# Four graph layers on one core: last rows as narrow products, a group's maxima in one reduction, exponentials one step earlier, the last output in quarters

## The chip, the core and the metric

The kernel runs on one core of a Trainium2 chip. The core has a matrix engine (PE, with a separate row PEld for the loading of its stationary operand), a vector engine (DVE), a scalar engine (ACT), GpSimd (POOL), and queues that issue DMAs, here mostly SyncE's (SP) and POOL's. Each engine works through its own list of instructions in order; semaphores hold an instruction back until what it reads is written and what it overwrites has been read. The metric is the device time in microseconds (us) of one execution, given as the median of several runs.

## The reference, cut to what matters

A graph of N = 2708 nodes with F = 512 features goes through four layers, each followed by `x = layernorm(x + layer(x))`. Layer 0 is a four-head attention with two dense blocks, and the change leaves it alone. The other three are:

```
# layer 1: mean over neighbours
A = (adj != 0);  deg = sum(A, axis=0)
y = A @ (x @ W + b) / deg[:, None]
# layer 2: masked softmax of x's own products
node_att = softmax(x @ node_w, axis=0)
h = x @ edge_w;  e = where(adj > 0, h @ h.T, -9e15)
y = adj * (node_att * softmax(e, axis=1)) @ (x @ weight) + bias
# layer 3: attention with a bias
a = (x@Wq+bq) @ (x@Wk+bk).T / sqrt(512) + adj + adj
y = softmax(a, axis=-1) @ (x @ Wv + bv)
```

All arrays are float32. 2708 is 21 blocks of 128 rows and one last block of 20, and this block of 20 is what several parts of the change are about.

## The kernel before

**Blocks and groups.** `BLOCKS` holds the 22 row blocks. Layer 1 works on four output blocks at a time (five groups of four, then one of blocks 20 and 21); layers 2 and 3 on `GROUPS` of three, seven of them, of which the last has four blocks (384 + 20 = 404 columns). A plain float32 product is two MATMUL instructions in the trace, one after the other; a product of `F32R` (layer 1's) is one.

**Layer 1** (L1013 to L1059). For every output group and every one of the 22 blocks jt of the sum, a strip of the transposed adjacency is loaded to `raw` (five buffers), turned to 0 and 1 in `at` (L1037, DVE), and used as the stationary operand of two products per output block (L1044), with `hid_hi` and `hid_lo`, the upper and lower part of the hidden rows. In the last group the strip is only 148 columns wide; the kernel zeroes `raw` first (L1033) and uses all 128 columns of the last block, of which 20 are real. When a group's sums are done, L1054 scales them and adds the old rows; the layer norms of these rows are put into the next group's loop, one every fourth jt. Those of the last group (blocks 20 and 21) come right after the loop (L1058).

**Between layers 1 and 2.** `quarters`, a small matrix that adds up four quarters of 32 partitions each, is made by 12 DVE additions (L1074 to L1083). Then layer 2's keys `hT` and values `sup` are projected group by group (L1430 to L1466), starting with transposes of the rows (L1095) that DVE copies out of PSUM (L1098).

**Layers 2 and 3** share `softmax_layer`. A step is one group and one block jt of keys. `one_score` loads the adjacency strip, makes the scores (L1203, 8 MATMULs; in layer 2, scores whose mirror image has been computed are transposed from a kept copy, L1195), masks or biases them on DVE into a tile `e` (L1497 or L1581) and takes the running maximum `mx` (L1251). For the block of 20 rows the four parts of the product go to four quarters of the array (L1227, `ps_parts`), are copied to SBUF (L1236) and added by a product with `quarters` (L1237). After a group's last score `spread_max` turns the maximum to one number per column: for each of the three or four blocks a transpose (L1263), a reduction (L1266) and a product with the identity (L1269), then a product with ones (L1274, `pb`) and a copy to `nmax` (L1287).

`one_sum` follows a score by `lag` = 25 steps: it adds `nmax` (L1294, DVE), takes the exponential (L1295, ACT), adds to the column sums `acc` (L1298 for the first block, a copy; L1305 for the others), in layer 2 multiplies by the adjacency, which is loaded again (L1500), and then gives `e` to PE for the output (L1310, in layer 2 six MATMULs; for the lonely last block L1339). After the last block `end` takes row sums of `acc` (L1360, `pr`), reciprocals (L1370) and, in layer 2, scales the result into the rows (L1505, L1506). `acc` has one buffer. Masks and adjacency strips share the five buffers of `a_cols`. The output sums take four PSUM banks in turn, three per group in layer 2.

In layer 3 `end` instead copies the sums out (L1356) and puts one `project` per output block into `later` (L1388, 8 MATMULs each), with `finish3` behind it: scale and add (L1587), layer norm (L102 to L112) and the store (L1592).

**Order.** A main loop (L1617 to L1634) calls, for each t, one score step, one sum step and one entry of `later`. Layer 3's scores start 12 steps after layer 2's have ended, so that for a while neither layer has a sum step. The instructions are not issued in this order alone: the framework plans ahead of time with estimated durations, gives every engine a fixed list, takes the earliest-written instruction that its plan holds to be ready, and adds the waits. Buffers with a tag are handed out in the order written, and a new use waits until the old one has been read.

Of the kernel before, what the change touches and what calls it, by code (L numbers as in the profile page):

```python
# [17 lines left out]
P = 128  # L18
# [11 lines left out]
def gnn_stack_kernel(  # L30
# [46 lines left out]
    rdeg = const.tile([P, NT], F32, name="rdeg")  # L77
    ones = const.tile([P, P], F32, name="ones")
    nc.vector.memset(ones, 1.0)

    def rows_tile(name):
        return big.tile([P, NT, F], F32, tag="rows", name=name)
# [863 lines left out]
    with (  # L946
# [66 lines left out]
        for g in range(0, NT, G):  # L1013
            group = range(g, min(g + G, NT))
            c0 = g * P
            w = min(N, c0 + G * P) - c0
            if g == G:
                ew_sb = load_weight(pw2, edge_w, "ew_sb")
                w2_sb = load_weight(pw2, w2, "w2_sb")
                nw_sb = load_row(pw2, node_w, "nw_sb")  # L1020
                b2_sb = load_row(pw2, b2, "b2_sb")
            pos = {
                it: psum.tile([P, F], F32, tag=f"po{it - g}", name="ps_nb", bufs=1 + (it - g < 2))
                for it in group
            }
            for jt, (j0, m) in enumerate(BLOCKS):
                if later and jt % 4 == 3:
                    y, n = later.pop(0)
                    layer_norm(y, y, n)
                raw = work.tile([P, G * P], F32, tag="raw", name="raw", bufs=5)  # L1030
                a = work.tile([P, G * P], F32R, tag="at", name="at", bufs=3)
                if m < P or w < len(group) * P:
                    nc.vector.memset(raw[:, : len(group) * P], 0.0)  # L1033
                for r in range(0, P if m == P else 2 * Q, P if m == P else Q):
                    nc.sync.dma_start(raw[r : r + m, :w], adjT[j0 : j0 + m, c0 : c0 + w])
                with tc.issue_after(ready[0].ins) if g == 0 and jt < 5 else nullcontext():
                    nc.vector.tensor_scalar(  # L1037
                        a[:, : len(group) * P], raw[:, : len(group) * P], 0.0, None, ALU.not_equal
                    )
                halves = (hid_hi, hid_lo) if m == P else (hid_hi,)  # L1040
                for it in group:
                    at = a[:, (it - g) * P : (it - g + 1) * P]
                    for k, half in enumerate(halves):
                        nc.tensor.matmul(  # L1044
                            pos[it],
                            at,
                            half[:, jt, :],
                            start=(jt == 0 and k == 0),
                            stop=(jt == NT - 1),
                        )  # L1050
            for it in group:
                n = BLOCKS[it][1]
                y = xs[:n, it, :]
                nc.vector.scalar_tensor_tensor(  # L1054
                    y, pos[it][:n], rdeg[:n, it : it + 1], y, ALU.mult, ALU.add
                )
                later.append((y, n))
        for y, n in later:  # L1058
            layer_norm(y, y, n)  # L1059

# [7 lines left out]
    GSPAN = [(g[0] * P, sum(BLOCKS[it][1] for it in g)) for g in GROUPS]  # L1070
    GW = max(w for _, w in GSPAN)
    GB = max(len(g) for g in GROUPS)

    quarters = featp.tile([P, C, Q], F32, name="quarters")  # L1074
    for c in range(C):
        nc.vector.tensor_tensor(
            quarters[:, c, :], ident[:, :Q], ident[:, Q : 2 * Q], ALU.add
        )
        for k in range(2, C):
            nc.vector.tensor_tensor(  # L1080
                quarters[:, c, :], quarters[:, c, :], ident[:, k * Q : (k + 1) * Q], ALU.add
            )
    quarters = quarters.rearrange("p c q -> p (c q)")  # L1083

    def key_tile(name):
        t = featp.tile([P, C, NFULL * P + Q], F32, tag="keys", name=name)
# [29 lines left out]
    def softmax_layer(  # L1116
# [12 lines left out]
        def key_order(gi):  # L1129

            late = list(range(NFULL // 2)) + [NT - 1] + list(range(NFULL // 2, NFULL))
            if not mirror:

                return late if gi else list(range(NT))
            early = [jt for jt in late if HOME[jt] < gi]
            late = [jt for jt in late if HOME[jt] >= gi]
            place = {jt: (k + 0.5) / len(early) for k, jt in enumerate(early)}
            place |= {jt: (k + 0.5) / len(late) for k, jt in enumerate(late)}
            return sorted(place, key=place.get)
# [113 lines left out]
        def spread_max(st):  # L1253

            gi = st["gi"]
            c0, w = GSPAN[gi]
            k = len(GROUPS[gi])
            tp = psum.tile([P, C, P], F32, tag="tp", name="tp_mx")
            nm = small.tile([P, GB], F32, tag="nm", name="nm")
            dg = att.tile([P, GB, P], F32, tag="dg", name="dg", bufs=1)  # L1260
            for b, it in enumerate(GROUPS[gi]):
                n = BLOCKS[it][1]
                nc.tensor.transpose(  # L1263
                    tp[:n, b, :], st["mx"][:, b * P : b * P + n], ident
                )
                nc.vector.tensor_reduce(  # L1266
                    nm[:n, b : b + 1], tp[:n, b, :], AX.X, ALU.max, negate=True
                )
                nc.vector.tensor_scalar(  # L1269
                    dg[:n, b, :n], ident[:n, :n], nm[:n, b : b + 1], None, ALU.mult  # L1270
                )
            pb = psum.tile([P, BANK], F32, tag="tp", name="pb")
            full = sum(BLOCKS[it][1] == P for it in GROUPS[gi])
            nc.tensor.matmul(  # L1274
                pb[:, : full * P],
                ones,
# [9 lines left out]
            st["nmax"] = att.tile([P, GW], F32, tag="nmax", name="nmax", bufs=2)  # L1286
            nc.scalar.copy(st["nmax"][:, :w], pb[:, :w])  # L1287

        def one_sum(st, k):
            gi, jt = st["gi"], st["order"][k]  # L1290
            c0, w = GSPAN[gi]
            j0, m = BLOCKS[jt]
# [1 line left out]
            nc.vector.tensor_tensor(e, e, st["nmax"][:, :w], ALU.add)  # L1294
            nc.scalar.activation(e, e, AF.Exp)  # L1295
            if k == 0:
                st["acc"] = att.tile([P, GW], F32, tag="acc", name="acc", bufs=1)
                nc.vector.tensor_copy(st["acc"][:, :w], e)  # L1298
                st["po"] = [
                    psum.tile([P, F], F32, tag=f"po{(GROUP * gi + b) % C}", name="po", bufs=1)  # L1300
                    for b in range(C if after is not None else len(GROUPS[gi]))
                ]
            else:
                acc = st["acc"][:m, :w]
                nc.vector.tensor_tensor(acc, acc, e[:m], ALU.add)  # L1305
            if weigh:
                weigh(e, load_a(gi, jt)[:, :w])

            def product(out, lhsT, rhs):
                nc.tensor.matmul(out, lhsT, rhs, start=(k == 0), stop=(k == NT - 1))  # L1310
# [37 lines left out]
        def end(st):  # L1348
# [19 lines left out]
            for b, it in enumerate(GROUPS[gi]):  # L1368
# [13 lines left out]
                if after is None:  # L1382
                    continue

                def project(b=b, it=it, n=n):
                    ps = psum.tile([P, F], F32, tag="tp", name="ps_o")
                    for c in range(C):
# [10 lines left out]

        states = {}

        def score_step(t):
            gi, k = divmod(t, NT)
            if k == 0:
                states[gi] = {"gi": gi, "e": [], "q": query(gi), "order": key_order(gi)}
            one_score(states[gi], k)
            if k == NT - 1:
                spread_max(states[gi])

        def sum_step(t):
            gi, k = divmod(t, NT)  # L1410
            if t == 0:
                last_values()
            one_sum(states[gi], k)
            if k == NT - 1:
                end(states.pop(gi))
# [10 lines left out]
    with (  # L1426
        tc.tile_pool(name="l2w", bufs=2) as work,
        tc.tile_pool(name="l2ps", bufs=4, space=PSUM) as psum,
    ):
        for gi, group in enumerate(GROUPS):  # L1430
            c0, w = GSPAN[gi]
            xt = work.tile([P, C, GW], F32, tag="xt", name="xt_g")
            for b, it in enumerate(group):
# [271 lines left out]
```

## Time and profile before

| what | value |
|---|---|
| median of 3 runs | 3321.99 us (3317.25 to 3322.62) |
| the profiled execution's own time | 3319.34 us |
| its span in the profile | 3317.5 us |
| PE busy | 3232.7 us (97%) |
| DVE busy | 1971.7 us (59%) |
| ACT busy | 1319.5 us (40%) |
| POOL busy | 130.1 us (4%) |

In the trace layer 1's sums run from 1293 to 1510 us of the span, the projections for layer 2 from 1511 to 1674, layer 2's steps from there to about 2398, and layer 3's from about 2310 to the end. The last MATMUL starts at 3311.4 us. A busy share is of the whole span; a MATMUL's duration includes its passage through the array, while the next one has already begun, so the distance between two starts tells more of PE than the duration. "Idle before" is the time the engine stood still before an instruction, and the arrow names the instruction that released it.

### The profile page before, as it was taken

The page shows a single profiled execution, that of the slowest core. Times are in us where ns is not written, and L with a number is a line of the kernel's source. Part 1 is how long each engine was busy: PE and PEld are TensorE (multiplying, and loading weights), DVE is VectorE, ACT ScalarE, POOL GpSimd, SP SyncE. Part 2 cuts the span into 40 slices and gives each one's busy share as a digit, 9 for nine tenths or more (in the row PEclk, how much of TensorE's full clock was granted, in tenths as well). Part 3 has the DMA queues.
Part 4 walks back from the last instruction along what each step waited for, and adds up shares of the span by engine and source line. Part 5 has one row for each costly group of instructions (what it writes and reads, how often), then busy time and mean ns, then how long its engine had stood idle before and what let it go on. Part 6 is the DMA issues. An engine that isn't in the chain of part 4 may idle for free.

```text
span 3317.5 us, 30401 instructions
## 1 busy us (share of the span) xinstructions
PE 3232.7 (97%) x10920; PEld 1725.2 (52%) x10920; DVE 1971.7 (59%) x3221; ACT 1319.5 (40%) x1497; POOL 130.1 (4%) x211
## 2 busy tenths in 40 slices
PE   8998999999999999999999999999999999999999
PEld 5443444454444446885554555444455555555554
DVE  7877977767687685445135667776353443543533
ACT  6887887457868652001133333332021010110111
POOL 1100100000000000000010000000000000000000
PEclk9999999999999999999999999999999999999999
DMA  8855863335555412540044444553211111111100
GB/s 289 299 189 169 310 214 123 105 108 199 177 176 175 161 40 84 144 123 15 1 127 128 119 124 134 148 148 108 69 46 34 42 34 42 40 32 45 36 24 20
DMA packets 172550, 381.45 MB, mean 115 GB/s; under 512 B 20938, under 2 KB 115094, under 8 KB 167982
## 3 DMA queue, kind: packets, MB, share of 16 engines
q1 hardware_dynamic: 156926, 308.16, 30.7%
q0 software_dynamic: 15472, 71.33, 5.8%
q8 instruction: 86, 1.41, 0.2%
q14 instruction: 66, 0.54, 0.1%
HBM read 307.22 MB, written 71.67 MB: 114 GB/s over the span
## 4 chain that ended last, share of the span: by engine, by line
PE 76%; DVE 9%; issue 8%; DMA 4%; ACT 3%; POOL 0%; SPq 0%; DVEq 0%; POOLq 0%; ACTq 0%
PE po L1310 22%; PE ps_s L1203 17%; PE po L460 11%; PE ps_nb L1044 6%; PE ps_wide L1105 4%; DVE t L393 3%; PE ps_hid L117 2%; PE ps_sup L1447 2%; PE ps_o L1388 2%; PE ps_mlp L713 2%; PE ps_dec L848 2%; DMA a<-adj_d 1%; ACT t L394 1%; DMA a_cols<-in_adjT_dram 1%; PE psm L483 1%
## 5 line engine op out<-in xcount | busy, mean ns | idle before, releaser
L393 DVE SCALAR_TENSOR_TENSOR t<-t,a 128x2708 f32<-128x2708 f32 (+1 forms) x156 | 462.1, 2974 | 125.0 <-ACT t L385 121.1
L385 ACT ACTIVATE t<-f1b,f2h 128x1354 f32<-128x1354 f32 (+1 forms) x312 | 428.1, 1413 | 61.7 <-PE po L460 28.0
L460 PE MATMUL po<-t,xw 128*128 128x452 f32 (+3 forms) x1056 | 415.1, 557 | 15.7 <-ACT t L394 15.7
L394 ACT ACTIVATE t<-t 128x2708 f32<-128x2708 f32 (+1 forms) x156 | 382.5, 2454 | 110.5 <-DVE t L393 110.3
L1310 PE MATMUL po<-sup,e 128*128 128x512 f32 x882 | 412.4, 602 | 6.2 <-DVE e L1500 5.9
L460 PE MATMUL po<-t,emb 128*128 128x452 f32 (+3 forms) x1056 | 400.3, 547 | 12.4 <-ACT t L394 9.1
L1310 PE MATMUL po<-e,xs 128*128 128x384 f32 (+1 forms) x1176 | 407.5, 489 | 0.0
L1203 PE MATMUL ps_s<-sup,hT 128*128 128x384 f32 (+1 forms) x1176 | 406.9, 490 | 0.0
L1581 DVE SCALAR_TENSOR_TENSOR e<-a_cols,ps_s 128x384 f32<-128x384 f32 (+1 forms) x154 | 85.6, 556 | 428.9 <-PE ps_s L1203 405.9
L460 PEld LDWEIGHTS po<-t,xw 128*128 128x128 f32 (+1 forms) x1056 | 191.2, 192 | 228.4 <-issue 201.7
L1203 PEld LDWEIGHTS ps_s<-sup,hT 128*128 128x128 f32 x1176 | 221.9, 190 | 164.2 <-issue 14.1
L460 PEld LDWEIGHTS po<-t,emb 128*128 128x128 f32 (+1 forms) x1056 | 193.5, 190 | 212.1 <-issue 187.3
L1310 PEld LDWEIGHTS po<-e,xs 128*128 128x128 f32 x1176 | 221.6, 190 | 157.2 <-issue 6.0
L1310 PEld LDWEIGHTS po<-sup,e 128*128 128x128 f32 x882 | 162.1, 192 | 173.9 <-issue 142.8
L1203 PE MATMUL ps_s<-hT 128*128 128x384 f32 (+5 forms) x672 | 212.3, 461 | 2.4 <-DVE e L1497 1.7
L97 ACT ACTIVATE ln_rstd<-ln_rstd 128x1 f32<-128x1 f32 x88 | 17.2, 201 | 495.0 <-DVE ln_rstd L96 494.7
L1496 ACT ACTIVATE a_cols<-a_cols,neg_big 128x384 f32<-128x384 f32 (+1 forms) x154 | 94.7, 616 | 239.0 <-DMA a_cols<-in_adjT_dram 190.7
L1044 PE MATMUL ps_nb<-hid_hi,at 128*128 128x512 f32 x484 | 185.6, 390 | 1.1 <-DVE at L1037 1.1
L1044 PE MATMUL ps_nb<-hid_lo,at 128*128 128x512 f32 x462 | 179.9, 389 | 0.0
L1305 DVE TENSOR_TENSOR acc<-acc,e 128x384 f32<-128x384 f32 (+2 forms) x294 | 162.4, 552 | 11.7 <-ACT e L1295 2.0
L1203 PEld LDWEIGHTS ps_s<-hT 128*128 128x128 f32 x672 | 122.4, 190 | 88.3 <-issue 17.3
L1294 DVE TENSOR_TENSOR e<-e,nmax 128x384 f32<-128x384 f32 (+1 forms) x308 | 154.5, 551 | 21.8 <-ACT nmax L1287 21.8
(247 smaller groups left out, 3316.8 us busy)
## 6 DMA issues: line engine op xcount, KB each, us to landing
a<-adj_d SPq DMA_DIRECT2D x110, 677.0 KB
a_cols<-in_adjT_dram SPq DMA_DIRECT2D x378, 192.0 KB
a<-in_adjT_dram SPq DMA_DIRECT2D x42, 677.0 KB
adj_d<-a POOLq DMA_DIRECT2D x42, 677.0 KB, 6.0
raw<-in_adjT_dram SPq DMA_DIRECT2D x105, 256.0 KB
kept<-t POOLq DMA_DIRECT2D x16, 1354.0 KB, 6.9
t<-kept SPq DMA_DIRECT2D x16, 1354.0 KB
a_cols<-in_adjT_dram SPq DMA_DIRECT2D x63, 202.0 KB
```

The costliest lines, as they stand in the source:

```text
L385: nc.scalar.activation(tv[:, k, :], f1b[:n, k, :w], AF.Tanh, bias=f2h[:n, jt, h : h + 1], scale=0.5,)
L393: step = nc.vector.scalar_tensor_tensor(tv, tv, GUARD, ab, ALU.add, ALU.mult)
L394: nc.scalar.activation(tv, tv, AF.Exp, scale=0.5)
L460: nc.tensor.matmul(po[HB * k + q][:, :qw], values[r : r + n, jt, h * P : (h + 1) * P], t[r : r + n, k, q0 : q0 + qw], start=(place == 0), ...
L1044: nc.tensor.matmul(pos[it], at, half[:, jt, :], start=(jt == 0 and k == 0), stop=(jt == NT - 1),)
L1105: nc.tensor.matmul(ps[:, :width], w(c, o), xt(c), start=(c == 0), stop=(c == C - 1),)
L1203: nc.tensor.matmul(ps[:, b * P : w], keys[:, c, j0 : j0 + P], st["q"][:, c, b * P :], start=(c == 0), stop=(c == C - 1),)
L1294: nc.vector.tensor_tensor(e, e, st["nmax"][:, :w], ALU.add)
L1305: nc.vector.tensor_tensor(acc, acc, e[:m], ALU.add)
L1310: nc.tensor.matmul(out, lhsT, rhs, start=(k == 0), stop=(k == NT - 1))
L1496: nc.scalar.activation(a, a, AF.Identity, bias=neg_big[: a.shape[0]], scale=1.0e30)
L1581: nc.vector.scalar_tensor_tensor(e, a, 2.0, ps, ALU.mult, ALU.add)
```

## The change

- **`quarters`** is made at the kernel's beginning, in the pool of constants, and no longer between layers 1 and 2.
- **Layer 1, last group.** `raw` is zeroed only for the last jt, `at` is made only as wide as the strip (148 columns), and block 21's products use its 20 columns as the stationary operand (128 rows by 20 columns) in place of 128.
- **Layer norms of blocks 20 and 21** after layer 1 are handed on as `last_rows` and issued before layer 2's second group of projections.
- **Key order of layer 3's first group:** the block of 20 comes last but one, not last.
- **`spread_max`:** all transposes first, then one reduction and one product with the identity for the full blocks together (and one of each for the block of 20). It is called after the first score of the next group; only the last group's comes straight after its last score.
- **`one_exp`** is split from `one_sum`: adding `nmax`, exponential, `acc` and the multiplication by the adjacency are issued for step t + 1 ahead of the products of step t, for the first step of a layer both. `acc` has two buffers.
- **Last output of layer 3:** block 21's projection is done in four quarters of the array (`project_parts`), copied by ACT and added by a product with `quarters` (`project_sum`); the order at the end becomes 18, parts of 21, 19, sum of 21, 20.

```diff
@@ constants @@
+    quarters = const.tile([P, C, Q], F32, name="quarters")
+    for c in range(C):
+        nc.vector.tensor_tensor(
+            quarters[:, c, :], ident[:, :Q], ident[:, Q : 2 * Q], ALU.add
+        )
...
@@ layer 1 @@
-                if m < P or w < len(group) * P:
-                    nc.vector.memset(raw[:, : len(group) * P], 0.0)
+                if m < P:
+                    nc.vector.memset(raw[:, :w], 0.0)
...
-                        a[:, : len(group) * P], raw[:, : len(group) * P], 0.0, None, ALU.not_equal
+                        a[:, :w], raw[:, :w], 0.0, None, ALU.not_equal
...
-                    at = a[:, (it - g) * P : (it - g + 1) * P]
+                    n = BLOCKS[it][1]
+                    at = a[:, (it - g) * P : (it - g) * P + n]
...
-                            pos[it],
+                            pos[it][:n],
...
-        for y, n in later:
-            layer_norm(y, y, n)
+        last_rows = later
@@ key_order @@
-                return late if gi else list(range(NT))
+                return late if gi else list(range(NFULL - 1)) + [NT - 1, NFULL - 1]
@@ spread_max @@
+            for b, count, n in [(0, full, P)] + [
+                (b, 1, BLOCKS[GROUPS[gi][b]][1]) for b in range(full, k)
+            ]:
+                some = slice(b, b + count)
                 nc.vector.tensor_reduce(
-                    nm[:n, b : b + 1], tp[:n, b, :], AX.X, ALU.max, negate=True
-                )
-                nc.vector.tensor_scalar(
-                    dg[:n, b, :n], ident[:n, :n], nm[:n, b : b + 1], None, ALU.mult
-                )
+                    nm[:n, some], tp[:n, some, :], AX.X, ALU.max, negate=True
+                )
+                nc.vector.tensor_tensor(
+                    dg[:n, some, :n],
+                    ident[:n, :n].unsqueeze(1).to_broadcast([n, count, n]),
+                    nm[:n, some].unsqueeze(2).to_broadcast([n, count, n]),
+                    ALU.mult,
+                )
@@ one_sum becomes one_exp and one_sum @@
-        def one_sum(st, k):
+        def one_exp(st, k):
...
-                st["acc"] = att.tile([P, GW], F32, tag="acc", name="acc", bufs=1)
+                st["acc"] = att.tile([P, GW], F32, tag="acc", name="acc", bufs=2)
                 nc.vector.tensor_copy(st["acc"][:, :w], e)
...
             if weigh:
                 weigh(e, load_a(gi, jt)[:, :w])
+
+        def one_sum(st, k):
...
@@ end, layer 3 @@
+                if it == NT - 1:
...
+                    def project_parts(b=b):
+                        ps = psum.tile([P, F], F32, tag="tp", name="ps_o4")
+                        for c in range(C):
+                            nc.tensor.matmul(
+                                ps[c * Q : (c + 1) * Q],
+                                oT[:, c, w - Q : w],
+                                after()[:, c, :],
+                                start=True,
+                                stop=True,
+                            )
+                        po = att.tile([P, F], F32, tag="values4", name="po4", bufs=1)
+                        nc.scalar.copy(po, ps)
+                        held.append(po)
+
+                    def project_sum(b=b, it=it, n=n):
+                        ps = psum.tile([P, F], F32, tag="tp", name="ps_o")
+                        nc.tensor.matmul(
+                            ps[:n], quarters[:, Q - REST : Q], held[0], start=True, stop=True
+                        )
+                        finish(it, ps[:n], rs[:n, b : b + 1])()
...
+                    before, last = later[-2:]
+                    later[-2:] = [project_parts, before, project_sum, last]
@@ score_step, sum_step @@
             one_score(states[gi], k)
-            if k == NT - 1:
+            if k == 0 and gi > 0:
+                spread_max(states[gi - 1])
+            if t == total - 1:
                 spread_max(states[gi])
...
             if t == 0:
                 last_values()
+                one_exp(states[0], 0)
+            if t + 1 < total:
+                one_exp(states[(t + 1) // NT], (t + 1) % NT)
             one_sum(states[gi], k)
@@ projections for layer 2 @@
         for gi, group in enumerate(GROUPS):
+            for y, n in last_rows if gi == 1 else ():
+                layer_norm(y, y, n)
```

## The prediction

> **What bounds the kernel now.** I read the page first.
>
> ```profile
> span 3317.5 us, 30401 instructions
> ...
> PE 3232.7 (97%) x10920; PEld 1725.2 (52%) x10920; DVE 1971.7 (59%) x3221; ACT 1319.5 (40%) x1497; POOL 130.1 (4%) x211
> ```
>
> PE is the bound and other engines count only where they make it wait, so an edit can earn in two ways: fewer or closer MATMULs, or a shorter PE wait. The chain of waits gives the steady distances: 8 MATMULs of 512 columns (L1388) in 3.43 us, 0.429 each; 32 of 384 (L1105) in 10.32, 0.322 each; 856 of layer 1's (L1044) in 194.59, 0.227 each. The width of the stationary operand is not in these numbers. Next, PE's own waits in 1670 to 2440 us (total, times, longest):
>
> ```profile
> PE po L1310 <- DVE e L1500: 5.9, 4, 3.9
> PE ps_s L1195 <- DVE e L1497: 2.3, 2, 1.9
> PE tp_mx L1263 <- DVE mx L1251: 1.7, 2, 1.3
> PE ps_s L1203 <- DVE e L1497: 1.7, 3, 0.9
> ```
>
> Few and small: what can be won is some 20 to 30 us of 3317. The timelines of PE and DVE show the longest one:
>
> ```profile
> 2282.13 0.72 PE L1360 MATMUL pr<-ones,acc 128*128 128x1 f32 x6
> 2286.78 3.78 PE L1310 MATMUL po<-sup,e 128*128 128x512 f32 x4 [3.93 <-DVE e L1500]
> ```
>
> ```profile
> 2283.32 2.06 DVE L1506 SCALAR_TENSOR_TENSOR xs<-po,rs,xs 128x512 f32<-128x512 f32 x3
> 2285.29 0.36 DVE L1298 COPY acc<-e 128x404 f32<-128x404 f32 x1
> ...
> 2286.17 0.56 DVE L1500 TENSOR_TENSOR e<-e,a_cols 128x404 f32<-128x404 f32 x1
> ```
>
> The next group's exponentials were long done, but `acc` has one buffer: its first copy must follow the old group's row sums (`pr`), DVE has put it behind L1506, and L1500 overwrites what the copy reads. PE then ran its next four MATMULs in 3.78 us, twice 0.429 apart: the wait also cost clock. The same view where layer 3's first maxima are taken:
>
> ```profile
> 2423.74 0.85 PE L1227 MATMUL ps_parts<-sup,hT 128*32 128x384 f32 x8
> 2425.19 0.91 PE L1237 MATMUL ps_s<-e,quarters 128*128 128x384 f32 x2 [0.60 <-ACT e L1236]
> 2427.42 0.30 PE L1263 MATMUL tp_mx<-ident,mx 128*128 128x128 f32 x1 [1.32 <-DVE mx L1251]
> ...
> 2430.09 1.62 PE L1274 MATMUL pb<-dg,ones 128*128 128x384 f32 x2 [0.80 <-DVE dg L1269]
> 2431.51 4.74 PE L1105 MATMUL ps_wide<-hT,mqk 128*128 128x384 f32 x8
> ```
>
> No sum steps exist here to fill PE, so each link of ACT, DVE and PE shows; again half clock follows. The step from layer 1 to 2:
>
> ```profile
> 1511.21 1.53 PE L1095 MATMUL tp<-ident,xs 128*128 128x128 f32 x12 [1.26 <-DVE xs L1054]
> 1515.32 1.98 PE L1447 MATMUL ps_sup<-w_sb,xt_g 128*128 128x512 f32 x4 [2.58 <-DVE xt_g L1098]
> ```
>
> Last, a place where a product with 20 columns stands between wide ones:
>
> ```profile
> 2399.88 0.91 PE L1203 MATMUL ps_s<-sup,hT 128*128 128x384 f32 x2
> 2400.72 1.03 PE L1376 MATMUL ps_po<-po,quarters 128*20 128x512 f32 x2
> 2401.68 8.01 PE L1203 MATMUL ps_s<-sup,hT 128*128 128x384 f32 x24
> ```
>
> The two L1203 lie between narrow products on both sides; they take 0.84 (2400.72 - 2399.88) in place of 2 x 0.322 = 0.64, and the narrow pair 0.96 in place of 0.86. Together 0.30 is lost for going narrow and back.
>
> **What the Trainium skill says.** "TensorEngine Tiling (Array Packing)", Key Properties: changing the tiling mode, not just the tile, drains the matrix engine. The trace agrees: start distances around L1376 and L1447's last block show +0.094 before a switch. "TensorE: Matmul & The Clock Gate", LDWEIGHTS: a load takes the operand's columns divided by 1.2, in ns, which would be 107 for 128 columns and 17 for 20 (estimates from that page); the trace has +0.105 on the first wide product after a narrow one and +0.014 on the first narrow one, so after a switch the load is not hidden. The same page, Part 1: an idle window halves PE's clock, and some 3.4 us of work restore it. After 2204 and 2286 the trace has doubled distances for 2.3 and 2.7 us in excess.
>
> **The change part by part.** Excess is the distance between two PE starts beyond the steady one.
>
> *Layer 1's narrow products.* The order per jt is wide, wide, narrow, narrow. 22 entries x (0.094 + 0.014) = 2.4; 21 returns x (0.093 + 0.105) = 4.2; together +6.5. No narrow F32R product is in the trace. Its distance could be a little below 0.227 (nothing is loaded for 108 columns; 43 x 0.01 = -0.4), and a switch might be hidden by F32R's single MATMUL, though L117, narrow, to L1044, wide, at 1292.99 shows the first F32R at 0.337 against 0.231 for those after it: +0.106. I take 0 for the first and the full switch. Bounds: -0.5 and +8. The 21 memsets that go (0.27 each, DVE) and narrower L1037 only help DVE; PE's two waits on it here (excess 0.69 at 1490.89, 0.76 at 1495.40) go, as a jt now lasts 1.2 us and not 0.9: -1.4. Sum **+5.1**.
>
> *Layer 1 to 2.* Between L1054's end (1511.2) and the first L1098 copy (1514.59) DVE does two layer norms and ten of the twelve small additions. Gone, the copy waits only for its four transposes (about 1511.8). PE needs its 12 transposes anyway (1.3 us); its 2.74 of excess shrink to near nothing. **-2.7** (bounds -1.5, -2.8). The wait for L1054 stays. The layer norms' new place is beside 19 us of PE work per group; uncovered they'd cost the same 2.7 again. The 12 additions at the start lie before 4.97 us, when PE's first product waits for a DMA, and the identity is there at 1.5: 0.
>
> *Group changes in layer 2.* Excess around the six changes: 0.3, 1.4, 1.3, 2.0, 6.2 (2204 to 2214, with half clock), 6.8 (2286 to 2292, likewise): 18.0. With two `acc` buffers and `one_exp` ahead, L1298 and L1500 of the new group stand before L1370, L1505 and L1506 on DVE; behind them wait only the scores' L1497 and PE's banks. What is late next: the new group's second product needs a bank that L1506's first (0.74, after 0.5 of small ones) frees, while PE has a score (0.33 to 2.6) and one product (0.86): about 0.5 per change, 3.0; and L1497, behind three L1506, still delays a score where scores are mere transposes, in three changes by about 1: 3.0. So -18.0 + 6.0 = **-12** (bounds -4, -17).
>
> *Maxima one score later.* Six small DVE operations of 0.29 become two, of which no row shows the shape; 384 elements are 0.55 in L1251, so 1.1 in place of 1.7. From transposes to L1500: transposes 0.5, reduce and product 1.1, `pb` 0.85, copy 0.48, L1294 0.55, L1295 0.52, L1298 0.35, L1500 0.55: 4.9, with queueing some 7. PE has three steps until it needs it (in the late groups 0.33 of L1195 and 2.57 of L1310 each, 8.7): hidden. At layer 2's first sums (1745, where L1500 was late by 1.27 already) scores alone cover it, and I charge **+1.5** (0 to +4).
>
> *Layer 3's first maxima.* Excess: 1.08 (L1237), 1.48, 0.58, 0.60, 1.17, then half clock 2.7: 7.6. Block 20's scores (2.6 us) now cover the ACT copy, L1105 and group 1's first score (12.9 us) the maximum. **-7.0** (bounds -4, -7.6). Layer 3's later groups have next to no excess: 0.
>
> *End.* 8 narrow MATMULs (3.43) become 8 in quarters, which in L1339 take 0.96, and 2 of the sum (0.86), plus a second switch 0.3: -1.2 on PE. But the last store has 128 rows: its packets end 1.66 us after issue, those of 20 rows 1.17: +0.5; and DVE has two blocks' chains (2.5 busy each) in the 4.6 us before the last one: +0.4. **-0.3** (-1.5, +1).
>
> Sum: 5.1 - 2.7 - 12 + 1.5 - 7.0 - 0.3 = -15.4. The execution profiled took 3319.34 (span 3317.5 and 1.8 around it): 3303.9. The median lies 2.65 above it: **3306.6**.
>
> **Rivals.** *The group changes keep their waits* (17 in 100): DVE's work there is nearly as much as before, and stalls at 1944, 2036 and 2123 name L1497, not L1500. Then layer 2 gives -2 and the sum is about -5: 3317. Against it: at 2286 no score is left, only L1500 holds PE. *The maxima come too late* (10 in 100, the slower side): slack falls from four steps to two before L1294. If the 7 us become 10 in late groups, and each of the six changes waits 3.5 and loses clock for 2.7 as at 2286, that is 37 in place of 18: +19, with the rest (-5) **3336**. It decides from about 3.8 us per change. For it: at 2272 to 2278 the way from first transpose to L1294 took 5.6. Against: a third of this was PE working on products between the single transposes, which the batch does away with. *More goes* (5 in 100): narrow switches hidden and all of layer 2's excess won, -26: 3296.
>
> **Numbers.** The likeliest case (68 in 100) has 3297 to 3315 by its bounds taken together. A measurement here tells about 0.2%, 6.6 us, from nothing: 3315.3 and 3328.6. Faster: 68 + 5 + a fifth of 17 = 0.76; same: the rest of 17, 0.14; slower 0.10. The range 3294 to 3321 leaves out the slow case and edges.
>
> **What will show it.** Layer 1's last group lasts 6 us longer, with first wide distances of 0.33; L1447 starts 1.3 us after L1095; no L1310 with idle over 1 us on L1500, no half clock after 2200; L1263 of layer 3's group 0 after L1105, without idle. Wrong if PE waits on `nmax`'s chain (L1294), if new rows of L1497 waits exceed 6 us, or if layer 1's last group keeps its 21 us.

## The result, and the profile after

| | before | after |
|---|---|---|
| median of 4 runs | 3321.31 us (3317.25 to 3322.62) | 3288.85 us (3285.64 to 3291.33) |
| the profiled execution's own time | 3319.34 us | 3290.97 us |
| its span | 3317.5 us | 3289.2 us |

The ratio is 0.9901, with an interval of 0.9888 to 0.9915: faster by 1%, some 32.5 us. The prediction had the direction, but 14.7 us of gain; the result lies below its range (3294). Nearest was the rival of 5 in 100, "more goes", with 3296.

The page of the kernel after has nearly the same PE work (11 us less busy time, two MATMULs more) in a span that is 28.3 us shorter (its last line here gives the share of each engine in the chain of work that ended last):

```profile
span 3289.2 us, 30359 instructions
...
PE 3221.7 (98%) x10922; PEld 1722.4 (52%) x10922; DVE 1944.6 (59%) x3144; ACT 1348.5 (41%) x1512; POOL 129.7 (4%) x211
...
PE 88%; DVE 5%; ACT 2%; DMA 2%; issue 1%; SPq 0%; DVEq 0%; ACTq 0%
```

Stages are compared by distances between two PE starts in the two traces. Layer 0 is the same work in both and scatters: 1204.8 us before, 1209.1 after, and from 1203.1 to 1209.1 over all kernels that are run below. So the comparison starts behind it, and from there on the two executions differ by 32.6 us, as the medians do.

| stage (from start to start of PE) | before | after | difference | predicted |
|---|---|---|---|---|
| layer 1, first five groups | 195.39 | 195.32 | -0.1 | 0 |
| layer 1, last group | 21.17 | 20.22 | -0.95 | +5.1 |
| layer 1's last product to layer 2's first score | 164.40 | 161.73 | -2.67 | -2.7 |
| from there to layer 2's first row sums | 167.84 | 166.40 | -1.44 | +1.5 |
| the six group changes of layer 2, row sums to row sums | 557.17 | 538.49 | -18.68 | -12 |
| layer 2's last row sums to layer 3's first sum | 55.16 | 47.93 | -7.23 | -7.0 |
| layer 3's sums | 842.59 | 841.44 | -1.15 | 0 |
| last sum to the end | 20.81 | 20.15 | -0.66 | -0.3 |

The six group changes, each with the sums of the group that follows, gave 0.19, 2.04, 2.46, 1.83, 6.16 and 6.00. PE's own waits in the stretch that answers to 1670 to 2440 of before (1670 to 2420 now; total, times, longest) name neither L1554 (the multiplication, L1500 before) nor L1264 (the transposes of the maxima, L1263 before):

```profile
PE ps_s L1237 <- ACT e L1236: 1.0, 1, 1.0
PE tp L1095 <- DVE ln_rstd L109: 0.7, 1, 0.7
...
PE ps_s L1203 <- DVE e L1551: 0.3, 1, 0.3
```

PE's timeline (start, busy time, instruction, output and operands, tiles, count) where layer 2's last group change was:

```profile
2268.79 0.72 PE L1374 MATMUL pr<-ones,acc 128*128 128x1 f32 x6
2269.38 5.40 PE L1324 MATMUL po<-sup,e 128*128 128x512 f32 x12
```

and DVE's there:

```profile
2267.64 0.56 DVE L1554 TENSOR_TENSOR e<-e,a_cols 128x404 f32<-128x404 f32 x1
...
2269.98 2.06 DVE L1560 SCALAR_TENSOR_TENSOR xs<-po,rs,xs 128x512 f32<-128x512 f32 x3
```

The next group's multiplications stand ahead of the old group's row sums. PE goes from `pr` straight into the next products, with twelve in 5.40 us; before it stood still for 3.93 and then ran four in 3.78. The bank that L1560 has yet to free costs at most 0.2 here: from the first of the twelve to the next product, at 2274.71, are 5.33 us, and 12 x 0.429 are 5.15. At the change before this one PE covers even that with the next score's transposes, which it puts between the group's first product and its second:

```profile
2193.33 0.72 PE L1374 MATMUL pr<-ones,acc 128*128 128x1 f32 x6
2193.92 0.69 PE L1195 MATMUL ps_s<-ident,s_kept 128*128 128x128 f32 x4
2194.53 1.13 PE L1324 MATMUL po<-sup,e 128*128 128x512 f32 x2
2195.50 0.49 PE L1195 MATMUL ps_s<-ident,s_kept 128*128 128x128 f32 x3
2195.82 1.88 PE L1324 MATMUL po<-sup,e 128*128 128x512 f32 x4
```

Where layer 3's first maxima are taken, the same view has three transposes between scores, all without idle time:

```profile
2402.61 0.91 PE L1105 MATMUL ps_wide<-hT,mqk 128*128 128x384 f32 x2
2403.36 0.83 PE L1237 MATMUL ps_s<-e,quarters 128*128 128x384 f32 x2
2404.03 2.74 PE L1203 MATMUL ps_s<-sup,hT 128*128 128x384 f32 x8
2406.61 9.84 PE L1105 MATMUL ps_wide<-hT,mqk 128*128 128x384 f32 x30
2416.28 2.74 PE L1203 MATMUL ps_s<-sup,hT 128*128 128x384 f32 x8
2418.86 0.49 PE L1264 MATMUL tp_mx<-ident,mx 128*128 128x128 f32 x3
```

From layer 1 to 2 only the wait for the last rows is left (the trace names a small memset of `hT` that DVE does as L1066, the scaling of these rows, ends). L1501 (L1447 before) starts 1.44 us after L1095, where it took 4.11:

```profile
1514.66 1.53 PE L1095 MATMUL tp<-ident,xs 128*128 128x128 f32 x12 [1.25 <-DVE hT L1087]
1516.10 1.98 PE L1501 MATMUL ps_sup<-w_sb,xt_g 128*128 128x512 f32 x4
```

And layer 1's narrow products, which the prediction charged for a switch of the array's mode at every change of width:

```profile
1495.80 0.39 PE L1056 MATMUL ps_nb<-hid_hi,at 128*20 128x512 f32 x1
1496.02 0.39 PE L1056 MATMUL ps_nb<-hid_lo,at 128*20 128x512 f32 x1
1496.25 0.39 PE L1056 MATMUL ps_nb<-hid_hi,at 128*128 128x512 f32 x1
1496.48 0.40 PE L1056 MATMUL ps_nb<-hid_lo,at 128*128 128x512 f32 x1
1496.72 0.39 PE L1056 MATMUL ps_nb<-hid_hi,at 128*20 128x512 f32 x1
```

Every distance shown is 0.22 to 0.24, whichever width comes next; the distance of 0.33 that was to follow each return isn't there. Over the whole group the only longer ones are the two at its single wait for DVE, at 1494.39 and 1495.23.

### The profile page after: what moved, and what is told of

Same layout as the page of the kernel before. It is cut to its first block, busy times and chain, and to the rows that moved or that the text cites. A ratio compares the mean times of both kernels' runs of the same rounds, so it can differ in the third digit from the quotient of the medians.

```text
span 3289.2 us, 30359 instructions
## 1 busy us (share of the span) xinstructions
PE 3221.7 (98%) x10922; PEld 1722.4 (52%) x10922; DVE 1944.6 (59%) x3144; ACT 1348.5 (41%) x1512; POOL 129.7 (4%) x211
## 4 chain that ended last, share of the span: by engine, by line
PE 88%; DVE 5%; ACT 2%; DMA 2%; issue 1%; SPq 0%; DVEq 0%; ACTq 0%
PE po L1324 23%; PE po L471 19%; PE ps_s L1203 18%; PE ps_nb L1056 6%; PE ps_wide L1105 4%; PE psm L494 3%; DVE t L404 2%; PE ps_hid L128 2%; PE ps_sup L1501 2%; PE ps_o L1432 2%; PE ps_mlp L724 2%; PE ps_dec L859 2%; DMA a<-adj_d 1%; ACT t L405 1%; ACT t L396 1%
## 5 line engine op out<-in xcount | busy, mean ns | idle before, releaser
L1302 ACT ACTIVATE e<-e 128x384 f32<-128x384 f32 (+1 forms) x308 | 151.7, 522 | 116.0 <-DVE e L1301 113.3
L1056 PE MATMUL ps_nb<-hid_hi,at 128*128 128x512 f32 x484 | 185.4, 390 | 0.4 <-DVE at L1048 0.4
L1056 PE MATMUL ps_nb<-hid_lo,at 128*128 128x512 f32 x462 | 179.9, 389 | 0.0
L108 ACT ACTIVATE ln_rstd<-ln_rstd 128x1 f32<-128x1 f32 (+1 forms) x88 | 17.2, 201 | 391.7 <-DVE ln_rstd L107 391.2
L1301 DVE TENSOR_TENSOR e<-e,nmax 128x384 f32<-128x384 f32 (+1 forms) x308 | 163.1, 552 | 23.3 <-ACT nmax L1294 23.3
```

Of the source, the lines that this page charges most:

```text
L1056: nc.tensor.matmul(pos[it][:n], at, half[:, jt, :], start=(jt == 0 and k == 0), stop=(jt == NT - 1),)
```

## The experiments

Two questions were open after the result. On layer 1: does a narrow float32r product leave the array's mode as it is, so that the switch is a matter of plain float32 (theory A), or do all narrow products switch, and layer 1 hid it (theory B)? On layer 2: did the single `acc` hold up the next group (theory C), or is it the exponential issued a step earlier that gains (theory D)? The rest takes the change apart. Six of the kernels (the first, and five variants of the change) have one run and no interval; for the five the stages of the trace are compared. Between kernels that share a stage these mostly agree to 0.1 us, in layer 1's last group to 0.3, and in the stretch up to layer 2's first row sums only to 0.95 (166.15 to 167.10), so that a difference there needs a wait in the trace beside it.

### The width of a product by itself

A kernel of its own: series of products of 128x512, with a wide and a narrow stationary operand by turns. Six of its 14 series, with comments added:

```
...
section(2, "rmix", r, r, 20, 16, pairs=2)    # float32r, 128 and 20 columns
...
section(4, "fmix", f, f, 20, 16)             # float32
...
section(6, "bmix", b, b, 20, 16, pairs=2)    # bfloat16
section(7, "fhundred", f, f, 100, 16)        # float32, 128 and 100 columns
...
section(9, "fwrn", f, r, 20, 16, pairs=1)    # float32 wide, float32r narrow
...
section(13, "fsixty", f, f, 64, 16)          # float32, 128 and 64 columns
```

> This kernel computes none of the layers: it runs series of 128 x 512 products on one tile of x, and writes a sum of them. Per series, wide (128 columns) and narrow (20) stationary operands alternate, in float32, float32r and bfloat16. Theory A (the switch belongs to the plain float32 product with its two MATMULs, and a float32r product of 20 columns leaves the array as it is): the float32r mix keeps 0.23 us from start to start throughout, the float32 mix loses 0.30 us per way out and back, as in the kernel before, and narrow float32r followed by wide float32 or the reverse loses only where the float32 one is narrow. Theory B (every product of 20 columns switches the array, and layer 1 only hid it behind its waits for the adjacency): the float32r mix loses 0.2 to 0.3 us per way out and back here too, where all operands lie ready. 100 columns in float32: no loss under both; 64 columns: a loss like that of 20. bfloat16 tells which of the two dtypes is the exception: no loss if it is float32 alone, 0.2 to 0.3 if it is float32r alone.

PE's timeline of this kernel, first the float32r series, then float32 (two MATMULs to a product), then bfloat16, each with two MATMULs of a width by turns:

```profile
46.51 0.63 PE L55 MATMUL narrow_rmix<-xr,lr 128*20 128x512 f32 x2
46.97 0.62 PE L55 MATMUL wide_rmix<-xr,lr 128*128 128x512 f32 x2
47.43 0.62 PE L55 MATMUL narrow_rmix<-xr,lr 128*20 128x512 f32 x2
...
88.18 1.04 PE L55 MATMUL narrow_fmix<-xf,lf 128*20 128x512 f32 x2
89.15 1.13 PE L55 MATMUL wide_fmix<-xf,lf 128*128 128x512 f32 x2
90.20 1.03 PE L55 MATMUL narrow_fmix<-xf,lf 128*20 128x512 f32 x2
...
124.76 0.60 PE L55 MATMUL narrow_bmix<-xb,lb 128*20 128x512 bf16 x2
125.29 0.60 PE L55 MATMUL wide_bmix<-xb,lb 128*128 128x512 bf16 x2
125.83 0.60 PE L55 MATMUL narrow_bmix<-xb,lb 128*20 128x512 bf16 x2
```

One period of float32r is 47.43 - 46.51 = 0.92 us, or 4 x 0.230, and alone a wide float32r product takes 0.227: 0.01 is lost in a whole period. One of float32 is 90.20 - 88.18 = 2.02, where four MATMULs at the 0.429 that both widths take alone would be 1.72: 0.30 for going narrow and back, what the prediction had read from L1376. One of bfloat16 is 1.07, where four at its 0.216 would be 0.86: 0.2. With 64 columns float32 pays a little more than with 20 (2.06 per period), with 100 nothing (0.429 a MATMUL). A float32 wide product with a float32r narrow one between keeps 1.087 per period, where the parts add up to 1.085; the reverse, float32r wide and float32 narrow, takes 1.39 and loses 0.31. A narrow product is no shorter than a wide one either (0.227 and 0.429 for series of narrow products alone).

The rows of PEld in the same trace show part of how. In the float32r series the load of a stationary operand starts one product ahead of the product that uses it (the first of these two at 46.74, its product at 46.97); in the float32 series the first load after a change of width starts only with its product (89.14 and 89.15):

```profile
46.74 0.42 PEld L55 LDWEIGHTS wide_rmix<-xr,lr 128*128 128x128 f32 x2
...
89.14 0.30 PEld L55 LDWEIGHTS wide_fmix<-xf,lf 128*128 128x128 f32 x2 [0.85 <-issue]
```

So what theory A says of layer 1 holds: narrow float32r products pay next to nothing, and layer 1 hid no price. But the switch isn't float32's alone, for bfloat16 pays too; float32r is the exception. Why it is stays open: the trace gives the rows and columns of a product, not the tiling mode that it asks for, so that a chip that treats float32r differently and an instruction that asks for the full width can't be told apart.

### A second buffer for `acc`, alone

```diff
-                st["acc"] = att.tile([P, GW], F32, tag="acc", name="acc", bufs=1)
+                st["acc"] = att.tile([P, GW], F32, tag="acc", name="acc", bufs=2)
```

> The kernel before with a second acc buffer and nothing else. Theory C (the single acc buffer is what held L1500 and with it PE at the changes of group): from layer 2's first score to its last row sums 13 to 17 us are saved of the 20.1 that the whole change saved there, the idle of 3.9 us before L1310 on L1500 is gone, and no half clock follows after 2200; in all -14. Theory D (it is issuing the exponentials a step ahead that does it, as the written order still puts the old group's end first): at most 5 us saved.

3305.56 us (3301.69 to 3307.83), a ratio of 0.9958 (0.9943 to 0.9973). The trace has layer 2 at 15.3 us less, of 20.1 in the whole change; the last two group changes give 4.90 and 6.00 of their 6.16 and 6.00. PE's waits in 1670 to 2440 of this kernel:

```profile
PE tp_mx L1263 <- DVE nm L1266: 1.8, 3, 1.1
PE tp_mx L1263 <- DVE mx L1251: 1.8, 2, 1.3
...
PE po L1310 <- DVE e L1500: 0.8, 1, 0.8
...
PE ps_s L1203 <- DVE e L1497: 0.5, 2, 0.3
```

The wait for L1500 is 0.8 in place of 5.9, and with it the waits for L1497 shrink (4.0 in two rows before, 0.5 in the one row left among the largest). One number in the code is worth about half of the whole gain: theory C.

### The step ahead with the second buffer

`one_exp` as in the change, on the kernel before with two `acc`, the maxima as they were:

```diff
+            if t == 0:
+                one_exp(states[0], 0)
+            if t + 1 < total:
+                one_exp(states[(t + 1) // NT], (t + 1) % NT)
             one_sum(states[gi], k)
```

> The kernel before with one_exp a step ahead and two acc buffers; maxima, layer 1 and the last output as before. Theory C: about what the second buffer alone gives, 14 to 18 us in layer 2, within 3 us of e2. Theory D: 15 to 20, and 10 or more beyond e2.

3299.57 us (3297.34 to 3300.63), a ratio of 0.9940 (0.9925 to 0.9955). Layer 2 is 19.6 us shorter than before, 4.3 more than with the buffer alone, which is somewhat beyond the 3 that were expected. The 4.3 lie at the first sums (1.3, where kernels scatter by nearly as much) and at the third to fifth change (0.4, 1.6, 1.3). Theory C keeps the larger part, but D isn't nothing.

### The maxima alone

The batch, the call after the next group's first score, and the key order of layer 3's first group, on the kernel before:

```diff
-                return late if gi else list(range(NT))
+                return late if gi else list(range(NFULL - 1)) + [NT - 1, NFULL - 1]
...
-            if k == NT - 1:
+            if k == 0 and gi > 0:
+                spread_max(states[gi - 1])
+            if t == len(GROUPS) * NT - 1:
                 spread_max(states[gi])
```

> The kernel before with the maxima in one reduction, behind the next group's first score, and layer 3's first key order; the rest as before. Theory C: in layer 2 only 2 to 4 us (fewer DVE operations, the wait of 0.6 for mx), between layer 2's last row sums and layer 3's first sum 7.2 us, in layer 3's later groups 1 us: -10 to -12 in all. A rival (layer 2's group changes suffered from DVE's small operations on the maxima): 8 or more in layer 2, -16 in all.

3308.66 us (3306.57 to 3309.78), a ratio of 0.9968 (0.9957 to 0.9979). In the trace: layer 2 -2.96, the way to layer 3's first sum -7.23, layer 3's sums -1.15, together -11.0 from layer 1 on. The last two are to the hundredth what the whole change shows, so this part is enough for them, and the others add nothing to it. (The second buffer alone shortens the way to layer 3's first sum as well, by 1.1, which is contained in the 7.23.) Layer 2's parts overlap too: 19.6 and 3.0 alone, 20.1 together. At the first sums nothing is lost (0.04), where the prediction charged 1.5.

### Layer 1's last group as it was

The change, but with wide products, `raw` zeroed and `at` made over 256 columns:

```diff
-                if m < P:
-                    nc.vector.memset(raw[:, :w], 0.0)
+                if m < P or w < len(group) * P:
+                    nc.vector.memset(raw[:, : len(group) * P], 0.0)
...
-                    n = BLOCKS[it][1]
+                    n = P
```

> The changed kernel with layer 1's last group as it was: 128 columns for block 21, and raw zeroed for every jt. Theory A (narrow float32r products cost and save nothing): the last group's products take 21.2 us again in place of 20.2, all of it PE's waits for DVE; nothing else moves. Theory B (the narrow product as such is the gain): also +1, but with start distances of wide products in the place of block 21 visibly longer than 0.23.

The group takes 21.39 us, 1.17 more than in the change, with the distances beyond 0.229 of 0.69 and 0.76 back that the kernel before has. The narrow products with all that belongs to them gain about 1 us. They don't cost 5.

### Narrow products, but the zeroing kept

```diff
-                if m < P:
-                    nc.vector.memset(raw[:, :w], 0.0)
+                if m < P or w < len(group) * P:
+                    nc.vector.memset(raw[:, : len(group) * P], 0.0)
```

with `at` again made over 256 columns, and the products 20 wide.

> The changed kernel with block 21's products still 20 columns wide, but raw zeroed for every jt and at made 256 wide as before. Theory A: 21.2 us, as in e5, for DVE's memsets are the whole difference. Theory B: 20.2 us stays.

21.68 us, 1.46 more than in the change, and as long as with wide products within the scatter of this stage. Both waits for DVE are here. On PE's timeline:

```profile
1493.97 0.50 PE L1056 MATMUL ps_nb<-hid_hi,at 128*128 128x512 f32 x1 [0.50 <-DVE at L1048]
...
1498.48 0.50 PE L1056 MATMUL ps_nb<-hid_hi,at 128*128 128x512 f32 x1 [0.57 <-DVE at L1048]
```

So what this part of the change gains is DVE's work that goes (21 zeroings and narrower comparisons, which weren't separated); the width of the products is worth nothing that these runs can tell.

### The two layer norms back at layer 1's end

```diff
-        last_rows = later
+        for y, n in later:
+            layer_norm(y, y, n)
...
-            for y, n in last_rows if gi == 1 else ():
-                layer_norm(y, y, n)
```

> The changed kernel with the layer norms of blocks 20 and 21 back at layer 1's end; quarters stays at the beginning. DVE's queue as the cause: from layer 1's last product to layer 2's first score 1.6 to 2.4 us of the 2.67 come back, the rest being the small additions. A rival (it was PSUM, which the old rows' L1054 frees): less than 0.5 comes back.

From layer 1's last product to the first score the way is 0.68 us longer than in the change, of the 2.67 that the change won: less than expected of the layer norms, and more than of the rival. PE's timeline and DVE's have the reason:

```profile
1512.26 1.53 PE L1096 MATMUL tp<-ident,xs 128*128 128x128 f32 x12 [1.26 <-DVE xs L1066]
1514.37 2.84 PE L1500 MATMUL ps_sup<-w_sb,xt_g 128*128 128x512 f32 x6 [0.58 <-DVE xt_g L1099]
```

```profile
1512.13 1.26 DVE L114 BATCH_NORM_STATS2 ln_st<-xs 128x6 f32<-128x512 f32 x2
...
1513.67 0.65 DVE L1099 COPY xt_g<-tp 128x512 f32<-128x512 f32 x1
1514.24 0.14 DVE L109 RECIPROCAL ln_rstd<-ln_rstd 128x1 f32<-128x1 f32 x1
```

Here the copy L1099 goes ahead of the layer norm's slow second half, and only the statistics hold it up. With the twelve additions there too, as before, it came after ten of them and both norms. So with the additions gone the norms cost 0.7, and the additions, with the place that the copy then had in DVE's list, made the other 2.0 of the 2.67. No run separates the two; DVE's timeline of before has 1.0 us from start to start for the ten additions and 0.9 for the two last operations of the norms (L112) ahead of the copy, so about half each, by that estimate.

### The batch, but straight after a group's last score

```diff
-            if k == 0 and gi > 0:
-                spread_max(states[gi - 1])
-            if t == total - 1:
+            if k == NT - 1:
                 spread_max(states[gi])
```

> The changed kernel with the maxima called straight after a group's last score, still in one reduction, and layer 3's new key order. Theory C: from layer 2's last row sums to layer 3's first sum 3 to 5 us of the 7.2 come back (PE stands for mx, the one reduction, the product and pb, and loses clock), in layer 2 less than 1.5, in layer 3's later groups nothing. A rival (the batch or the key order alone did it): less than 1 comes back.

The way to layer 3's first sum is 3.74 us longer, as expected; layer 2 is 0.8 longer, and layer 3's sums 2.24, where nothing was expected. PE's timeline at layer 3's first maxima:

```profile
2402.98 2.74 PE L1203 MATMUL ps_s<-sup,hT 128*128 128x384 f32 x8
2407.06 0.52 PE L1264 MATMUL tp_mx<-ident,mx 128*128 128x128 f32 x3 [1.33 <-DVE mx L1251]
2408.91 0.88 PE L1281 MATMUL pb<-dg,ones 128*128 128x384 f32 x2 [1.33 <-DVE dg L1274]
2409.63 10.48 PE L1105 MATMUL ps_wide<-hT,mqk 128*128 128x384 f32 x32
```

The chain of transposes, reduction, product and `pb` is short now, but PE has nothing of its own between the links: 1.33 before the first and 1.33 before the last. Behind the next score (2418.86 above) the same three transposes wait for nothing. So of the 7.23 the place is worth 3.74, and batch and key order the rest, which no run divides. In layer 3's later groups the gain is the place's alone: without it the batch is slower than the kernel before (843.68 against 842.59), with it faster (841.44).

### The last output in whole products

The change without `project_parts` and `project_sum`: block 21's projection is eight MATMULs again, in their old order.

> The changed kernel with the last output in four whole products again, the order 18, 19, 20, 21. The prediction's terms (PE -1.2, the larger last store +0.5, DVE's second chain +0.4) give 0.3 us; the comparison of the profiles gives 0.66 from layer 3's last sum to the end. If the terms are right except DVE's, this run ends 0.6 to 0.8 us later than the changed kernel from that point, PE's last start 1.2 later.

From the last sum to the end it takes 20.81 us, 0.66 more, and exactly what the kernel before has. The last MATMUL starts 1.17 later, and the time from there to the end is 0.51 shorter: PE's -1.2 and, on the way from there to the end, the +0.5 that was charged to the larger store. The +0.4 for two blocks' chains on DVE isn't there, as DVE's timeline of the kernel after shows:

```profile
3282.57 0.53 DVE L123 TENSOR_SCALAR sup<-sup,ln_mv,ln_rstd 20x512 f32<-20x512 f32 x1
3283.12 0.75 DVE L1641 SCALAR_TENSOR_TENSOR sup<-ps_o,rs,sup 128x512 f32<-128x512 f32 x1
```

Block 21's chain has just ended when the last product's sum is ready: L1641 starts 0.63 us after the last MATMUL's start, where its like took 0.69 before.

### The change without the step ahead

```diff
-                one_exp(states[0], 0)
-            if t + 1 < total:
-                one_exp(states[(t + 1) // NT], (t + 1) % NT)
+            one_exp(states[gi], k)
```

> The changed kernel with one_exp called for step t just before the products of step t (two acc buffers, maxima and all else as changed). Theory C, with e2 and e3 in hand (15.3 us by the buffer, 4.3 more by the step ahead): layer 2 gets 2 to 5 us of its 20.1 back, at the changes into the fourth and fifth group above all; layer 3 nothing; the time stays below 3296. If the later maxima need the step ahead to be hidden, or the reverse, more: layer 2 gets 8 or more back.

3291.11 us (3289.68 to 3292.94), a ratio of 0.9913 (0.9895 to 0.9931), which by times alone isn't told from the change. By stages layer 2 is 3.0 us longer, of which 1.74 at the first sums, where less was expected, and 0.22 and 0.94 at the fourth and fifth change; layer 3 is the same. PE's timeline of this kernel at the first sums has the wait that the kernel before has there (1.10 at 1745.45):

```profile
1743.55 0.81 PE L1203 MATMUL ps_s<-hT 128*128 128x384 f32 x2
1745.29 2.84 PE L1324 MATMUL po<-sup,e 128*128 128x512 f32 x6 [0.94 <-DVE e L1552]
```

and the kernel after has none at this place:

```profile
1744.13 0.81 PE L1203 MATMUL ps_s<-hT 128*128 128x384 f32 x2
1744.77 2.74 PE L1324 MATMUL po<-sup,e 128*128 128x512 f32 x6
```

## Why the prediction was right and wrong

Five terms missed, and all to the same side: 6.0 (layer 1), 6.7 (group changes), 2.9 (first sums), 1.2 (layer 3's sums) and 0.4 (the end) are 17.2, the way from the -15.4 of its sum to the -32.6 measured.

**Layer 1's narrow products, +5.1: wrong in mechanism.** The step that failed carried the +0.094, +0.014 and +0.105 of float32 products (L1376, L1447) over to the float32r products of L1044 (L1056 now). The trace of before had no narrow float32r product, and the prediction said so, took the full switch nevertheless, and named as support the 0.106 on the first float32r product after L117. That one follows a narrow *float32* product: at most it shows that leaving that mode costs, not that a narrow float32r product enters it. Nor is the figure a mark of a switch alone: the same 0.335 to 0.337 stand in the trace of before behind both waits for DVE (1490.89 and 1495.40), between products that all have 128 columns. Its bounds for the switch reached down to -0.5, and with no switch its other term, -1.4 for PE's two waits, remains. The measured -0.95 is that, with one of the two waits kept (0.61 and 0.11 beyond the steady distance at 1494.39 and 1495.23). Of the prediction's own signs of being wrong this is the one that nearly came: the group was to keep its 21 us, and took 20.22.

The Trainium skill's "TensorEngine Tiling (Array Packing)", Key Properties, which the prediction leant on, says that changing the mode drains the engine, and the float32 and bfloat16 series agree with it (0.523 and 0.31 before each change of width, in place of 0.429 and 0.216); that 128x20 float32r products behave as no change of mode is this measurement's. The prediction's other reading, that the load isn't hidden after a switch, is borne out by the rows of PEld above; the loads themselves take 0.19 and 0.10 us in these traces for 128 and 20 columns, not the 107 and 17 ns of the prediction's estimate.

**Group changes in layer 2, -12: right in mechanism, wrong in size.** The reason given was the right one, as the second buffer alone shows (-15.3 in layer 2). What failed was "what is late next": 3.0 for the bank and 3.0 for L1497. The measured -18.7 is all of the 18.0 of excess and a little more; buffer and step ahead alone give -17.9 there. The bank wait was covered, at the two changes shown, by the next score's transposes or but for 0.2 by products ahead of it; and L1497's waits were not an independent cost but followed from the same hold-up, as they all but went when only the buffer was added. Of the stalls at 1944, 2036 and 2123 that name L1497, which the prediction put on the rival's side, the first two changes lost 1.86 and 1.62 with the buffer alone; the third gave 0.10 with it and 1.68 with the step ahead as well.

**Maxima one score later, +1.5: wrong in sign.** -1.44 at layer 2's first sums. The maxima cost nothing there (0.04 in the run with them alone), and the step ahead takes the late L1500's 1.1 us away (back as 0.94 without it). The prediction counted the step ahead only at the group changes. How much of the 1.44 is scatter isn't known; the wait that goes is in the traces.

**Layer 3's first maxima, -7.0: right** (-7.23), and for its reason: the run with the maxima alone has the same. **Layer 1 to 2, -2.7: right in size** (-2.67), and DVE's queue was the cause, but the shares weren't as they seemed: the norms alone are 0.7 of it.

**Layer 3's later groups, 0:** -1.15, about 0.2 per change, from the maxima. **End, -0.3:** -0.66; the second chain on DVE was in time. (The prediction's own figures for PE, 3.43 - 0.96 - 0.86 - 0.3, give 1.3 and not the 1.2 that it put down; 1.17 was measured, so the slip did no harm.)

Of the rivals, "the group changes keep their waits" and "the maxima come too late" are both out by the traces: no PE wait names the multiplication or `nmax` among the largest. "More goes" had 5 in 100 and both of its halves came true, though float32r's switch wasn't hidden, as it had it, but absent. It should have had more, and its sum was taken too small: with a layer 1 of -1.4 and an excess of 18.0 all won, the prediction's own numbers come to 5.1 + 1.4 + 6.0 = 12.5 below its 3306.6, or 3294.

## What to carry to other kernels

Take a price from a row of the same data type, or hold it open on both sides with weight: one small series of products would have settled it. Where an in-place consumer shares a single-buffered accumulator with the group before, look for all the waits that hang on it before charging any of them as staying; here one more buffer won about half of the change. And look for a place for a chain of small steps over several engines behind work that needs none of it: here the place hid it, while making it short left 1.33 us open at two of its links as long as nothing stood between.

## What the hardware showed that was not expected

- A stationary operand of 20 columns costs 0.30 us for the way out and back among wide float32 products, 0.20 among bfloat16 ones, and next to nothing among float32r ones (0.230 a product, 0.227 alone). With 100 columns float32 pays nothing. With 64 it costs 0.34.
- Between a bfloat16 or float32 narrow product and a float32r narrow one the switch is paid (0.309 and 0.327 as start distances, 0.09 and 0.10 beyond the steady ones, each seen once, between two series), as if the float32r one were wide.
- The narrower stationary operand shortens no product: 0.227 us for float32r and 0.429 for a float32 MATMUL of 512 columns, at 20 columns as at 128.
